# A three-layer graph convolution: each node's first 14 edges taken as lists by indirect fetches, in place of a search on TensorE and VectorE

## The chip, the cores and the metric

The kernel runs on one core of one Trainium2 chip. The metric is the device time of one execution in microseconds, and a kernel is stated by the median of its runs.

## The reference

6,250 nodes carry 256 features each. 100,000 edges (src, dst), sorted by dst, are the same in all three layers.

```python
deg = segment_sum(1, dst) + 1                 # the +1 is a node's own loop
dinv = rsqrt(deg)
h = x
for W, b in ((W1, b1), (W2, b2), (W3, b3)):   # 256 -> 512 -> 512 -> 256
    h = relu(segment_sum((h @ W)[src] * dinv[src] * dinv[dst], dst) + own loop + b)
out = layernorm(x + h)
```

The kernel aggregates before it multiplies by W, so that a layer gathers rows of its input table by src and sums them by dst.

## The kernel before

**Tiling.** The nodes are 50 blocks of 125 (`Q`); a block owns about 2,000 edges. A stage that counts comes first (the loop over `counted(g)`, ten blocks at a time): for each block it finds where each node's edges begin in the sorted list (`n_below`), the degrees, and dinv. Then three layers follow. In each, some blocks are *dense*: a matrix of edge counts between the block and each of the 50 source blocks, in uint8, is turned to float and multiplied with the table that lies in SBUF as two halves (`parts`). The other blocks are *gathered*: indirect fetches on the queue of GpSimd (POOL) bring the source rows of their edges.

**First layer** (`first_layer`). Blocks 0 to 20 are dense (L1453, 50 matmuls to a block). Blocks 21 to 49 are gathered, 16 fetches of 128 edges to a block and one row of rest edges for ten blocks (L1368). For blocks 26 to 45 the table holds both halves of a row, and a fetch lands in a slot of `split` (`SPLIT_ROWS[0]` of them, two more lent); for the others it lands in one of eight rows of `room`. The sum over edges is a matmul with a one-hot matrix (`product`, L1402; 17 to a block, 493 in all). Four one-hot matrices are made by one VectorE instruction (`more_hots`, L1324) into a tile of the pool `onehot`. One *chunk* is one fetch with all that the builder lays beside it; chunk c issues fetch c and multiplies what fetch c-5 brought (c-7 in the tail, from block 46 on).

**What else runs in the chunks of the first layer.** All of it is generators that are stepped once a chunk at build time, so that the order on each engine is fixed:

- `counts`: makes the uint8 matrices of blocks 0 to 25: one-hot pairs on VectorE (L1038), a matmul (L1111), a copy on ScalarE (L1072). It takes an accumulator bank from the shared list `common` when more than `SPARE` are in it.
- `after1`: turns, multiplies by W1, and stores a block's result to the table of layer 1 (L1673, L1705, L1713).
- `finding` (`all_found`): the numbers of the edges that the second and third layer fetch, for blocks 16 to 49, two blocks at a time. `found_rounds` computes `round_src`, the src of each node's first 14 edges (`ROUNDS`): a matmul that spreads the degrees (L600), a Sign on ScalarE, four matmuls with steps of the numbers (L609), a copy, and eight VectorE instructions (L617 to L632). `found_beyond` computes the numbers of the edges past the 14th. Both take a bank of `common`. `rows_risen` makes the steps they use.
- `caching`: once 20 dense blocks are done, loads the stored table of layer 1 into `parts`, two blocks every four chunks (L83).
- `teams`: blocks 0 to 15 of the second layer, dense, four at a time, 1,600 matmuls (L1197). They may start in the tail of the first layer when `counts` has stored 26 blocks and `found_beyond` is done, and go on in the second layer, where a goal per chunk steps them.

**Second and third layer** (`layer`). A gathered block has 14 fetches by `round_src`, one row per node, that VectorE adds up (L1631), and a few past them with one-hot matmuls (L1587). All are issued on POOL at L1571, 599 in the second layer and 317 in the third.

**Early in the program**, a step of `windows` also fetches from the edge list on POOL (L729) and VectorE reads the result at L736; `in_parts` then splits the rows of x that have been scaled by dinv (L899 on ScalarE, L900 on VectorE), and frees rows of `room` for the first fetches.

Of the kernel before, what the change touches and what calls it, by code (L numbers as in the profile page):

```python
# [10 lines left out]
F32 = mybir.dt.float32  # L11
# [3 lines left out]
I32 = mybir.dt.int32  # L15
# [23 lines left out]
SPLIT_ROWS = (7, 4, 7)  # L39
# [4 lines left out]
SPARE = 0  # L44
# [23 lines left out]
FIRST_EDGES = TEAM * TEAMS  # L68
G = 5
# [334 lines left out]
def sorted_path(ctx: ExitStack, tc: tile.TileContext, x, edges, starts, found, wts, biases, room, late, out):  # L404
# [41 lines left out]
    degs, before = ends[:Q], more[:Q]  # L446
# [55 lines left out]
    nodes_later = finder.tile([P, Q], BF16, name="elater")  # L502
    marks = [finder.tile([P, LANES], BF16, name=f"emarks{n}") for n in range(2)]
    less = finder.tile([P, KF], F32, name="eless")
    count_of = finder.tile([P, NE], BF16, name="ecount")
    low_of = finder.tile([P, NE, 2], BF16, name="elow")
    over_of = finder.tile([P, NE], BF16, name="eover")
    ends_of = finder.tile([P, NE], F32, name="eends")
    rises = finder.tile([P, NE, 2, 2 * KF + 1], BF16, name="erises")
    row_steps = [scratch[:, at:at + P // 2].bitcast(BF16) for at in (1456, 1984)]  # L510
# [4 lines left out]
    run = finder_room[:Q, 476:476 + 4 * KF].rearrange("p (b j) -> p b j", b=2)  # L515
    rounds_ready, beyond_ready = set(), set()

    def finder_numbers(spare):
# [11 lines left out]
        own, by, end_rows = spare[:, 2:5], spare[:, 5:7], spare[:, 7:8]  # L530
# [4 lines left out]
        nc.vector.tensor_scalar(nodes_later, number[:, :Q], part, None, op0=ALU.is_gt)  # L535
# [3 lines left out]
        nc.vector.tensor_single_scalar(by[:, 0:1], part, 1.0, op=ALU.add)  # L539
        nc.vector.tensor_single_scalar(by[:, 1:2], part, -1.0, op=ALU.add)  # L540
        nc.vector.tensor_scalar(eye, number, part, None, op0=ALU.is_equal)
        nc.vector.tensor_scalar(other, number, by[:, 0:1], None, op0=ALU.is_equal)
        nc.vector.tensor_sub(row_steps[0], eye, other)
        nc.vector.memset(eye[:, 0:1], 0.0)
        nc.vector.tensor_scalar(other, number, by[:, 1:2], None, op0=ALU.is_equal)
        nc.vector.tensor_sub(row_steps[1], other, eye)
# [32 lines left out]
    def rows_risen():  # L579

        for n in range(2):
            for b in range(0, NE, 16):
                of = slice(b, min(NE, b + 16))
                bank = yield from one_of_common(0)
                risen = bank[:, :(of.stop - b) * 2 * KF]
                nc.tensor.matmul(risen, lhsT=row_steps[n], rhs=bits[:, of].rearrange("p b k j -> p (b k j)"), start=True, stop=True)
                yield 1
                for k in range(2):
                    nc.scalar.activation(rises[:, of, k, 1 + n * KF:1 + (n + 1) * KF],
                                         risen.rearrange("p (b k j) -> p b k j", k=2, j=KF)[:, :, k], AF.Copy, scale=0.5)  # L590
# [1536 lines left out]
```

## Time and profile before

| | us |
|---|---|
| median of 3 runs | 2172.53 (2168.84 to 2179.11) |
| the profiled execution: its time | 2180.69 |
| the profiled execution: its span | 2178.6 |

| engine | busy us | share of the span |
|---|---|---|
| TensorE (PE) | 1877.0 | 86% |
| TensorE weight loads (PEld) | 1429.2 | 66% |
| VectorE (DVE) | 1584.5 | 73% |
| ScalarE (ACT) | 1120.9 | 51% |
| GpSimd (POOL) | 1437.7 | 66% |

The granted TensorE clock is a mean of 0.93 of full speed. Times in the views count from the span's start. The counting stage ends at about 88 us, where the first fetch of a table row is issued; the first layer's fetches end at 860 us, the second layer's start at 878 us. A row of the timeline gives the start, the duration, engine, line, what is written from what, the count of merged instructions, and in brackets how long the engine sat idle before and what ended it. A PE duration is modelled and overlaps the next matmul. "issue" is a short idle time that nothing in the profile explains. `w_sb` in the views is `scratch`, `st` a block's result, `sacc`, `smm`, `str`, `mat_ps`, `win_ps` the accumulator banks.

### The profile page before, as it was taken

What the parts mean: (1) busy time and instruction counts of PE and PEld (TensorE: products, weight loads), DVE (VectorE), ACT (ScalarE), POOL (GpSimd) and SP (SyncE); (2) the same over time, 40 slices, a digit from 0 to 9 for tenths busy, and PEclk for the clock granted to TensorE, in tenths of its full rate; (3) what the DMA queues carried; (4) which work ended last, traced back from release to release, by engine and by line L of the source; (5) the groups of instructions that cost most, each with busy time, mean ns of one, the idle gap of its engine ahead of it and who ended that gap; (6) DMA issues with size and microseconds to landing.
All of it is one profiled execution on the core that took longest, in us unless ns stands there. A gap on an engine that the chain in (4) does not pass through costs nothing.

```text
span 2178.6 us, 29385 instructions
## 1 busy us (share of the span) xinstructions
PE 1877.0 (86%) x8610; PEld 1429.2 (66%) x8610; DVE 1584.5 (73%) x3148; ACT 1120.9 (51%) x2138; POOL 1437.7 (66%) x1426
## 2 busy tenths in 40 slices
PE   3479999999999668789888997899886899999996
PEld 2366766666666346568666886678665677777775
DVE  6777777787876746667677676767666478888876
ACT  1566666777676445444434443434443455556552
POOL 2254655665666556677777777777774477777775
PEclk6599999999999779989999999999898999999998
DMA  7675677878879974777777777777788567787774
GB/s 165 185 220 182 174 209 199 219 208 209 215 212 265 306 206 140 222 201 222 216 223 208 216 220 204 215 220 217 210 228 227 153 167 206 199 208 206 201 211 135
DMA packets 226047, 449.46 MB, mean 206 GB/s; under 512 B 44089, under 2 KB 103426, under 8 KB 225876
## 3 DMA queue, kind: packets, MB, share of 16 engines
q0 software_dynamic: 117840, 303.15, 50.9%
q1 hardware_dynamic: 92196, 132.48, 21.8%
q10 hardware_dynamic: 15840, 11.86, 2.2%
q8 instruction: 69, 1.13, 0.2%
q14 instruction: 102, 0.84, 0.1%
HBM read 374.97 MB, written 69.81 MB: 204 GB/s over the span
## 4 chain that ended last, share of the span: by engine, by line
PE 43%; DMA 21%; DVE 13%; issue 9%; POOL 6%; ACT 4%; SPq 0%; ACTq 0%; POOLq 0%; DVEq 0%
DMA room<-tab,round_src 10%; POOL room L1571 6%; PE smm L1654 5%; PE sacc L1453 4%; DMA room<-tab,over_src 4%; PE sacc L1654 4%; PE str L1654 4%; DVE room L1038 4%; DMA room<-tab,efirst_src 2%; PE sacc L1402 2%; DMA halves<-both,efirst_src 2%; DVE total L1631 2%; PE smm L1789 2%; PE sacc L1587 1%; PE sacc L1705 1%
## 5 line engine op out<-in xcount | busy, mean ns | idle before, releaser
L1571 POOL DMA_INDIRECT room<-tab,round_src x728 | 762.4, 1047 | 280.1 <-issue 138.6
L1631 DVE TENSOR_TENSOR total<-total,room 125x512 f32<-125x512 f32 (+1 forms) x694 | 410.4, 591 | 116.6 <-DMA room<-tab,round_src 105.9
L1368 POOL DMA_INDIRECT halves<-both,efirst_src x304 | 286.9, 944 | 194.9 <-PE sacc L1402 51.9
L1038 DVE TENSOR_TENSOR room<-near_cols,slots 128x625 bf16<-128x625 f32 (+2 forms) x390 | 295.0, 802 | 28.0 <-PE sacc L1111 13.3
L1168 ACT CAST dense_rows<-parts 125x512 fp32r<-125x512 f32 x200 | 123.8, 619 | 252.8 <-PE near_cols L1197 250.5
L1571 POOL DMA_INDIRECT room<-tab,over_src x182 | 192.3, 1056 | 60.7 <-issue 29.6
L1368 POOL DMA_INDIRECT room<-tab,efirst_src x144 | 146.4, 1017 | 103.5 <-PE sacc L1402 28.8
L1170 DVE TENSOR_TENSOR dense_rows<-parts,dense_rows 125x512 fp32r<-125x512 f32 x200 | 137.9, 689 | 105.6 <-ACT dense_rows L1168 104.2
L1274 ACT CAST piece<-room 125x625 fp32r<-125x625 uint8 x217 | 152.2, 714 | 109.5 <-PE smm L1654 30.8
L1197 PE MATMUL sacc<-dense_rows 125*125 125x512 f32 x400 | 146.7, 441 | 60.6 <-DVE dense_rows L1170 25.9
L1453 PE MATMUL sacc<-parts,dense_rows 125*125 125x512 f32 x600 | 192.7, 428 | 2.7 <-ACT dense_rows L1274 2.5
L1623 ACT CAST halves<-room 128x512 fp32r<-128x512 f32 (+1 forms) x188 | 101.5, 545 | 173.5 <-DMA room<-tab,over_src 152.1
L1274 ACT CAST dense_rows<-room 125x625 fp32r<-125x625 uint8 x210 | 150.2, 719 | 38.0 <-PE sacc L1453 23.3
L1626 DVE TENSOR_TENSOR halves<-room,halves 128x512 fp32r<-128x512 f32 (+1 forms) x188 | 110.5, 597 | 69.1 <-ACT halves L1623 67.8
L1654 PE MATMUL smm<-parts,piece 125*125 125x512 f32 x550 | 141.7, 410 | 0.0
L1111 PEld LDWEIGHTS <-room 128*125 128x125 bf16 x650 | 89.3, 144 | 77.8 <-issue 47.4
L1197 PE MATMUL win_ps<-dense_rows 125*125 125x512 f32 x400 | 138.3, 428 | 1.5 <-DVE room L1750 1.5
L1197 PE MATMUL mat_ps<-dense_rows 125*125 125x512 f32 x400 | 138.5, 428 | 1.1 <-DVE room L1750 1.1
L1324 DVE TENSOR_TENSOR shot<-near_cols,edlo 128x500 fp32r<-128x500 f32 x108 | 72.8, 674 | 89.6 <-PE sacc L1402 45.9
L1197 PE MATMUL near_cols<-dense_rows 125*125 125x512 f32 x400 | 135.0, 419 | 1.9 <-DVE room L1750 1.9
L1654 PE MATMUL sacc<-parts,piece 125*125 125x512 f32 x505 | 127.6, 405 | 8.9 <-DVE piece L1274 8.9
L1197 PEld LDWEIGHTS sacc<-dense_rows 125*125 125x125 f32 x400 | 73.9, 191 | 91.5 <-DVE dense_rows L1170 35.8
(503 smaller groups left out, 4268.2 us busy)
## 6 DMA issues: line engine op xcount, KB each, us to landing
kept<-room SPq DMA_DIRECT2D x32, 683.6 KB
room<-kept SPq DMA_DIRECT2D x32, 683.6 KB
tab<-st SPq DMA_DIRECT2D x60, 224.0 KB
parts<-tab SPq DMA_DIRECT2D x29, 448.0 KB
room<-tab,round_src POOLq DMA_INDIRECT x728
both<-parts SPq DMA_DIRECT2D x10, 1120.0 KB
room<-kept SPq DMA_DIRECT2D x160, 68.4 KB
room<-in_x SPq DMA_DIRECT2D x50, 112.0 KB
```

Of the source, the lines that this page charges most:

```text
L1038: nc.vector.tensor_tensor(out, numbered[0][:, :shape[2]].unsqueeze(1).to_broadcast(shape), numbers.unsqueeze(2).to_broadcast(shape), op=AL ...
L1168: nc.scalar.copy(to[:, :HID], row)
L1170: nc.vector.tensor_sub(to[:, HID:], row, to[:, :HID].bitcast(F32))
L1197: nc.tensor.matmul(team_banks[n][:Q], lhsT=team_pieces[u % 2][:, n, :], rhs=both_parts[u % 2][:, h * HID:(h + 1) * HID], start=(u % NB == ...
L1274: convert(piece, matrix[:, c * PIECE:(c + 1) * PIECE, :])
L1368: nc.gpsimd.indirect_dma_start(out=row, out_offset=None, in_=table, in_offset=bass.IndirectOffsetOnAxis(ap=at, axis=0))
L1453: nc.tensor.matmul(acc_d[:Q], lhsT=got[done // PIECE][:, k % PIECE, :], rhs=parts[:, k], start=(k == 0), stop=(k == NB - 1))
L1571: nc.gpsimd.indirect_dma_start(out=row, out_offset=None, in_=tables[i], in_offset=bass.IndirectOffsetOnAxis(ap=at, axis=0))
L1623: nc.scalar.copy(two[:, :width], landed[chunk - hi_lag])
L1626: nc.vector.tensor_sub(two[:, width:], landed.pop(chunk - lo_lag), two[:, :width].bitcast(F32))
L1631: nc.vector.tensor_add(own, parts[:, b].bitcast(F32) if i == 1 and r == 0 else own, landed.pop(chunk - ADDED[i])[:Q])
L1654: nc.tensor.matmul(acc_d[:Q], lhsT=got[done // PIECE][:, k % PIECE, :], rhs=parts[:, k], start=(k == 0), stop=(k == NB - 1))
```

## The change

`n_below` already says where a node's edges begin, so the src numbers of its first 14 edges stand in 14 consecutive entries of the edge list. The changed kernel computes that place (`ask`) and fetches 28 words (14 pairs of src and dst) for each of the 125 nodes of a block with one indirect fetch (`asked`), 34 fetches in all. The first 18 blocks' lists are fetched in the counting stage into a tile of their own, the other 16 after the last fetch of the first layer, into a part of `room` that `found_beyond` used. `listed` turns lists into `round_src` with three VectorE instructions for many blocks. `found_rounds`, the tiles it needed, and half of `rows_risen` go. In the space that this frees the pool `onehot` has a third buffer and `split` in the first layer an eighth slot. `SPARE` goes from 0 to 1: `counts` leaves one bank in `common`.

```diff
-SPLIT_ROWS = (7, 4, 7)
+SPLIT_ROWS = (8, 4, 7)
-SPARE = 0
+SPARE = 1
+ASKED = 18
...
-    run = finder_room[:Q, 476:476 + 4 * KF].rearrange("p (b j) -> p b j", b=2)
+    late_lists = finder_room[:Q, :(NE - ASKED) * 2 * ROUNDS].bitcast(I32).rearrange("p (b r t) -> p b r t", r=ROUNDS, t=2)
...
     def rows_risen():
-        for n in range(2):
-            for b in range(0, NE, 16):
...
+        for b in range(0, NE, 16):
...
-    def found_rounds(e):
...
+    def asked(of, lists, first):
+        for e in of:
+            nc.gpsimd.indirect_dma_start(
+                out=lists[:, e - first].rearrange("p r t -> p (r t)"), out_offset=None, in_=edges,
+                in_offset=bass.IndirectOffsetOnAxis(ap=ask[:Q, e:e + 1], axis=0))
+
+    def listed(of, lists):
+        n = len(of)
+        es, bs = slice(of.start, of.stop), slice(FIRST_EDGES + of.start, FIRST_EDGES + of.stop)
+        real = scratch[:Q, 1536:1536 + n * ROUNDS].rearrange("p (b r) -> p b r", r=ROUNDS)
+        nc.vector.tensor_tensor(real, cols[:Q, :ROUNDS].unsqueeze(1).to_broadcast([Q, n, ROUNDS]),
+                                degs[:, bs].unsqueeze(2).to_broadcast([Q, n, ROUNDS]), op=ALU.is_lt)
+        nc.vector.scalar_tensor_tensor(real, lists[:, :n, :, 0], -float(N), real, op0=ALU.add, op1=ALU.mult)
+        nc.vector.tensor_single_scalar(round_src[:Q, es], real, float(N), op=ALU.add)
+        rounds_ready.update(of)
...
     def all_found():
         yield from rows_risen()
-        ahead = 1
-        for n in range(len(pairs_found) + ahead):
-            if n < len(pairs_found):
-                yield from found_rounds(pairs_found[n])
-            if n >= ahead:
-                yield from found_beyond(pairs_found[n - ahead])
+        for e in range(0, NE, 2):
+            yield from found_beyond(e)
...
+        lists = dp1.tile([Q, ASKED, ROUNDS, 2], I32, name="elists")
...
-                nc.scalar.copy(before[:, gs], n_below[:Q])
+                nc.vector.tensor_tensor(ask[:Q, es], n_below[:Q, skip:], line[:Q, g + skip:g + GRP], op=ALU.add)
+                asked(range(es.start, min(es.stop, ASKED)), lists, 0)
...
-                nc.scalar.copy(count_of[:Q, es], deg_ps[:, 1, skip:])
...
             bits_of(ed, find_space)
+            listed(range(ASKED), lists)
...
-    onehot = one.enter_context(tc.tile_pool(name="sonehot", bufs=2))
+    onehot = one.enter_context(tc.tile_pool(name="sonehot", bufs=3))
...
                 if chunk < total:
                     gather(chunk)
+                if chunk == total:
+                    asked(range(ASKED, NE), late_lists, ASKED)
...
     def last_weights():
+        listed(range(ASKED, NE), late_lists)
         load_w2()
```

How the order changes is shown at three places. In the changed file the first layer's lines stand 34 lower than before and the second layer's 32 lower: the gathers of L1368 are L1334, the products of L1402 are L1368, the teams of L1197 are L1163, L1571 is L1539, and the fetch of L729 is L692.

The first place is POOL's queue at the end of the counting stage, before the change (`ed` is the edges of a block, `room` the rows of the first table fetches, `w_sb` the window fetch):

```order
L774 DMA ed<-in_edges 128x32
L729 DMA w_sb<-in_edges,w_sb 125x256
L1368 DMA room<-tab_170,rest 128x256
L1368 DMA room<-tab_170,efirst_src 128x256 x36
L729 DMA w_sb<-in_edges,w_sb 125x256
L1368 DMA room<-tab_170,efirst_src 128x256 x44
```

The same place of POOL's queue after the change:

```order
L739 DMA ed<-in_edges 128x32
L590 DMA elists<-in_edges,eask 125x28 x18
L692 DMA w_sb<-in_edges,w_sb 125x256
L1334 DMA room<-tab_170,rest 128x256
L1334 DMA room<-tab_170,efirst_src 128x256 x36
L692 DMA w_sb<-in_edges,w_sb 125x256
```

The 18 list fetches stand ahead of the first window fetch, and so of all fetches of table rows.

The second place is POOL's queue where the first layer ends and the second begins, before the change:

```order
L1368 DMA halves_968<-both,efirst_src 128x512
L1368 DMA room<-tab_170,efirst_src 128x256 x64
L1571 DMA room<-tab_171,round_src 128x512 x14
L1571 DMA room<-tab_171,rest 128x512
L1571 DMA room<-tab_171,over_src 128x512 x4
```

The same place after the change:

```order
L1334 DMA halves_983<-both,efirst_src 128x512
L1334 DMA room<-tab_170,efirst_src 128x256 x64
L590 DMA room<-in_edges,eask 125x28 x16
L1539 DMA room<-tab_171,round_src 128x512 x14
L1539 DMA room<-tab_171,rest 128x512
```

The 16 late list fetches stand between the last gather of the first layer and the first of the second.

The third place is TensorE where the teams' matmuls begin in the tail of the first layer (`halves` are the fetched rows, `shot` the one-hot matrices, `dense_rows` the teams' operands). Before the change, with 428 products ahead of the first team row:

```order
L1402 MATMUL sacc_986<-halves_970,shot 125x512
L1402 MATMUL sacc_986<-halves_971,shot 125x512
L1197 MATMUL sacc_984<-dense_rows 125x512 x2
L1197 MATMUL win_ps<-dense_rows 125x512 x2
L1402 MATMUL sacc_986<-halves_966,shot 125x512
L1197 MATMUL mat_ps<-dense_rows 125x512 x2
```

After the change, with 454 products ahead of it:

```order
L1368 MATMUL sacc_999<-halves_982,shot 125x512
L1368 MATMUL sacc_999<-halves_983,shot 125x512
L1163 MATMUL mat_ps<-dense_rows 125x512 x2
L1368 MATMUL sacc_999<-halves_984,shot 125x512
L1163 MATMUL str<-dense_rows 125x512 x2
L1163 MATMUL win_ps<-dense_rows 125x512 x2
```

The teams begin 26 products later. Counted over the whole order up to the second layer's first matmul of W2, 302 team matmuls stand there, 372 before. Ahead of product 384 stand 998 dense matmuls of L1453 and 534 of the counting matmuls of L1111; before they were 1,050 and 575. The 1,000th dense matmul, after which `caching` may load, stood at product 366 before, with 550 counting matmuls ahead of it.

84 lines of the change are left out of this document (19 added, 65 removed).

## The prediction

> **What bounds the kernel now.** I read the stages first. These are rows of the windows view: busy time of each engine in a stretch (instructions in brackets), then the granted clock, the share of the DMA engines and their rate.
>
> ```profile
> core 0: us, PE busy (x) PEld busy (x) DVE busy (x) ACT busy (x) POOL busy (x), PEclk, DMA share, GB/s
> 95.00:200.00 105.00, 83.58 (x435) 63.08 (x435) 83.07 (x166) 64.99 (x128) 56.47 (x58) 0.88 0.74 228
> 200.00:640.00 440.00, 413.61 (x2228) 297.59 (x2227) 338.45 (x720) 303.51 (x585) 255.77 (x270) 0.99 0.76 201
> 640.00:700.00 60.00, 57.21 (x268) 41.79 (x267) 44.62 (x73) 41.87 (x73) 40.69 (x43) 1.00 0.98 264
> 700.00:800.00 100.00, 63.43 (x215) 38.85 (x213) 57.69 (x96) 43.89 (x85) 56.26 (x60) 0.76 1.05 265
> 800.00:877.00 77.00, 69.46 (x265) 50.36 (x266) 47.92 (x97) 47.18 (x108) 45.37 (x42) 0.96 0.55 150
> 877.00:1650.00 773.00, 679.93 (x2883) 535.49 (x2881) 547.22 (x847) 329.96 (x617) 596.22 (x569) 0.95 0.75 217
> ```
>
> The search that goes runs between 113 and 580 us, in the first layer. There TensorE is occupied 94% of the time (413.61 of 440) at full clock, and everything else has room. POOL issues a fetch every 1.63 us (440 over 270). From 700 us on the picture turns: DMA is full (1.05), TensorE has 37 us free in 100. In the second layer POOL sets the pace: 773 over 569 is 1.36 us to an instruction, close to the 1.25 between the starts of two undisturbed fetches (877.73 and 878.98, below). So a microsecond of TensorE's work is worth a microsecond up to about 700 us, and little behind that.
>
> Next, who waits for whom between 200 and 640 us; columns are total, times, longest, in us. The largest waits of VectorE and of TensorE:
>
> ```profile
> DVE shot L1324 <- PE sacc L1402: 30.9, 19, 3.9
> DVE shot L1324 <- PE mat_ps L1402: 10.0, 6, 2.9
> DVE shot L1324 <- PE str L1402: 9.9, 4, 3.9
> ...
> PE win_ps L1705 <- DVE st L1710: 4.9, 3, 3.3
> PE sacc L1673 <- DVE st L1710: 4.1, 2, 2.8
> PE win_ps L1111 <- ACT room L1072: 2.8, 2, 2.5
> PE sacc L1111 <- ACT room L1072: 2.6, 5, 1.4
> ```
>
> VectorE stands 51 us (three rows) before a one-hot tile whose buffer a product still reads, with everything queued behind it. TensorE's own waits are small, 14.4 us in these four rows: VectorE's stalls mostly wait for an engine that is late anyway.
>
> **The change, part by part.** *Search removed, TensorE.* What a matmul costs in the stream is the distance between starts:
>
> ```profile
> 300.69 0.28 PE L600 MATMUL str<-elater,ecount 125*128 125x125 bf16 x2
> 300.81 0.27 PE L1111 MATMUL win_ps<-room 128*125 128x250 bf16 x1
> 300.92 0.27 PE L1111 MATMUL smm<-room 128*125 128x250 bf16 x1
> 300.94 0.94 PE L1453 MATMUL sacc<-parts,dense_rows 125*125 125x512 f32 x3
> 301.72 0.39 PE L1402 MATMUL sacc<-dense_rows,shot 128*125 128x512 f32 x1
> 301.95 0.87 PE L1453 MATMUL sacc<-parts,dense_rows 125*125 125x512 f32 x3
> ...
> 302.89 0.19 PE L609 MATMUL str<-erises,eones 128*125 128x66 bf16 x1
> 302.92 0.22 PE L609 MATMUL str<-erises,ereached 128*125 128x66 bf16 x1
> ...
> 303.09 0.41 PE L1111 MATMUL win_ps<-room 128*125 128x250 bf16 x2
> ```
>
> Two of L600 take 0.12 us (300.69 to 300.81), four of L609 0.20 (302.89 to 303.09): 0.32 a pair of blocks, 17 pairs, 5.4 us. Three matmuls of `rows_risen` add under 1. I take 6. By durations it would be 17 x (2 x 0.14 + 4 x 0.22), about 20 us, and the gain 14 larger. I take the starts, because 0.22 lies over the next matmul in each of these rows. The Trainium skill, page "Perfetto Trace Analysis", section "Identifying the Most-Contended Engine", says likewise that matmul busy time misleads since instructions are pipelined; by that rule too the small figure is the one to use.
>
> *Search removed, VectorE and ScalarE.* One pair's eight instructions:
>
> ```profile
> 122.65 0.16 DVE L617 SCALAR_TENSOR_TENSOR eoff<-egot,more 125x2 f32<-125x2 f32 x1 [4.64 <-ACT egot L613]
> 122.72 0.23 DVE L618 SCALAR_TENSOR_TENSOR room<-egot 125x64 f32<-125x64 f32 x1
> ...
> 123.09 0.62 DVE L624 TENSOR_TENSOR w_sb<-room,ebegin 125x448 f32<-125x448 f32 x1
> ...
> 124.81 0.81 DVE L1038 TENSOR_TENSOR room<-near_cols,slots 128x625 bf16<-128x625 f32 x1
> ```
>
> That is 2.16 us (122.65 to 124.81), 37 us over 17 pairs, plus two ScalarE instructions each. Neither engine bounds the stage (338 and 304 of 440), so this counts only through TensorE's waits for them, under the buffers.
>
> *A spare bank.* With one bank left in the list, counting takes fewer chances. By the order, ahead of product 384 stand 52 dense matmuls and 41 counting matmuls fewer than before. At 0.26 (three of L1453 from 300.94 to 301.72) and 0.11 that is 13.5 + 4.5 = 18 us that leave the stretch where TensorE bounds and fall into the next 65 products, where it has 37 us of 100 free. I count the whole 18 as gained; if the tail takes them badly, half, 9. The teams, squeezed at the end, leave 70 matmuls (372 less 302), again 18 us, to the second layer. I count 2 there, because POOL bounds it and TensorE is free 12% (679.93 of 773); the ends are 0 and 18.
>
> *Third one-hot buffer, eighth slot.* The 51 us of VectorE stalls go for the most part. What is late next is TensorE itself, so of its 14.4 us I take half, 7; the ends are 0 and 14.
>
> *Early list fetches.* POOL's rows around the first table fetch and at the seam of the layers, a small indirect fetch from the same list (L819, a group of five: busy, mean ns), VectorE's `n_below` (L863) of blocks 20 to 29 and 30 to 39, and its use of L729:
>
> ```profile
> L819 POOL DMA_INDIRECT rest<-in_edges,place_i x5 | 4.8, 969 | 1.5 <-issue 1.2 <-DVE w L534 0.3
> 58.07 0.17 DVE L863 SCALAR_TENSOR_TENSOR n_below<-full_ps,n_part 126x10 f32<-126x10 f32 x1
> 69.57 0.17 DVE L863 SCALAR_TENSOR_TENSOR n_below<-full_ps,n_part 126x10 f32<-126x10 f32 x1
> 73.55 1.24 POOL L729 DMA_INDIRECT w_sb<-in_edges,w_sb  x1 [41.76 <-DVE w_sb L726]
> 79.59 0.22 DVE L736 TENSOR_SCALAR w_sb<-w_sb 125x128 f32<-125x128 int32 x1
> 87.94 3.31 POOL L1368 DMA_INDIRECT room<-tab,rest  x1 [13.15 <-DVE parts L900]
> ...
> 859.57 1.00 POOL L1368 DMA_INDIRECT room<-tab,efirst_src  x1 [0.30 <-issue]
> 877.73 0.94 POOL L1571 DMA_INDIRECT room<-tab,round_src  x1 [17.16 <-DMA parts<-st]
> 878.98 0.95 POOL L1571 DMA_INDIRECT room<-tab,round_src  x1 [0.30 <-issue]
> ```
>
> A list fetch costs POOL 0.97 + 0.30 = 1.27 us, or 1.54 if it is like L729. From 58.5 us ten run to 71.2, then four to 76.3, and L729 behind them starts 2.8 later than 73.55 (6.5 at the higher price). It had ended at 74.8 and was used without a wait at 79.59, so between 0 and 6.5 us reach VectorE, and by it `parts` and the first fetch; I take 1.2. `listed` adds three instructions of 252 columns, between 0.23 (L618) and 0.62 (L624) each: 0.7 to 1.9, I take 1.2. The four small VectorE additions and eight ScalarE copies of the counting stage cancel.
>
> *Late list fetches.* POOL idles from 860.6 to 877.7 for the last store. Sixteen at 1.27 take 20.3 us from 860.9 to 881.2: 3.5 us beyond the gap, 7.8 at the higher price, 0 if the gap widens. The second layer's rows for them are needed 18 blocks later, so `listed` there hides.
>
> *Sum:* -6 -18 -7 +2 +1.2 +1.2 +3.5 = -23 us against the profiled execution's 2180.7, of which 2178.6 is the span. That execution lies 8 above the median of 2172.5; the same difference on the median gives 2149.5, said as 2149.
>
> **The rivals.**
>
> *The tail keeps its length.* The loads of layer 1's table start when 1,000 dense matmuls are done:
>
> ```profile
> 681.49 0.79 SPq L83 DMA_DIRECT2D parts<-tab  x2
> ```
>
> From there to 877.73 are 196 us, with DMA full. That start moves from product 366 to 384, so TensorE's work up to it hardly falls: 18 products more at 0.23 (301.72 to 301.95), 16 counts less, the search's 6 less, about -4. With waits -7 and the additions of +8 the time is 2172.5 - 3, about 2170. For it speaks the DMA share of 1.05; against it that behind the later start only some 101 fetches remain in place of 121, and that rows of half the width come sooner.
>
> *TensorE's clock falls in the tail (slower).* In 700 to 800 us TensorE is idle for 37% and granted 0.76; in 800 to 877 the teams hold it at 0.96. The teams now start 26 products later. If the stage at 800 to 877 gets the clock of the one before it, its 69.46 us of work grow by 0.96/0.76, 18 us, and with the tail keeping its length the time is 2170 + 18 = 2188. It decides where the granted clock of the last 77 us falls below about 0.85; against it stand the delayed counts, which fill the same stretch. The Trainium skill, page "TensorE: Matmul & The Clock Gate", section "What's actually happening", has the clock at half after an idle window of about 3.4 us; the trace agrees in that 0.76 goes with the idle stretch.
>
> *All waits go.* TensorE's 14 us of waits vanish, and the teams' 18 us leave the tail as well: -6 -18 -14 -18 +8 = -48, 2124. Against it: landing fetches, not TensorE, hold the tail.
>
> **How the numbers follow.** Forecast 0.58, tail keeps its length 0.18, clock 0.13, all waits go 0.11. The forecast's own ends (half of the 18, no waits saved, both list prices high; or all waits saved and no cost at the seams) reach from about 2133 to 2167. The range takes in the first and third rival and leaves out most of the clock's: 2115 to 2178. A measurement of this kernel tells about 0.5%, 11 us, from no change. Faster by more than that, below 2161.6: nearly all of the forecast, 0.54, the third rival, 0.11, and some of the first, 0.05: 0.70. Slower: the clock, 0.13. The same: 0.17.
>
> **What would show it.** Right: POOL's fetches between 200 and 640 us come about 1.5 us apart; the waits of `shot` are nearly gone; the first table fetch stands at about 90 us; POOL's list fetches at the seam end 3 to 4 us after the point where the store would have let it go; the second layer's pace stays 1.36. The first load stands only some 10 us earlier, the first fetch of the second layer some 25. Wrong: the last fetch of the first layer not earlier than 850 us, a granted clock below 0.85 in the tail, or a second layer longer by 10 us.

## The result, and the profile after

The changed kernel takes 2108.53 us (median of 4 runs, 2099.89 to 2117.84), the kernel before 2174.1 in the same runs: a ratio of 0.970, 95% interval 0.965 to 0.975. That is faster, as forecast, but by some 65 us where 23 were forecast, and below the low end of 2115. The profiled execution took 2117.84, the longest of the four; its span is 2116.1 against 2178.6.

The stages first, in the windows view of the changed kernel (columns as before):

```profile
core 0: us, PE busy (x) PEld busy (x) DVE busy (x) ACT busy (x) POOL busy (x), PEclk, DMA share, GB/s
95.00:200.00 105.00, 80.64 (x478) 60.83 (x478) 84.02 (x164) 66.20 (x129) 59.83 (x57) 0.84 0.72 226
200.00:640.00 440.00, 437.45 (x2265) 324.16 (x2264) 338.44 (x641) 325.45 (x593) 301.65 (x319) 1.00 0.86 233
700.00:800.00 100.00, 70.02 (x250) 48.06 (x250) 69.18 (x139) 58.48 (x135) 63.04 (x61) 0.79 0.74 204
743.00:820.00 77.00, 62.97 (x238) 46.26 (x238) 37.87 (x75) 41.93 (x91) 50.22 (x44) 0.87 0.59 156
820.00:1593.00 773.00, 688.94 (x2932) 547.92 (x2932) 555.61 (x861) 339.36 (x632) 599.17 (x571) 0.95 0.76 218
```

Between 200 and 640 us TensorE is now occupied for 437 us of 440, where it was 414, and POOL issues 319 fetches there in place of 270: 1.38 us to a fetch, not 1.63. The second layer keeps its pace (571 POOL instructions in 773 us, before 569). The stretch from 743 to 820 us is the last ahead of the second layer, as 800 to 877 was before.

In the waits view of the changed kernel, 200 to 640 us, these four rows are all that TensorE waited for, 2.4 us, where the same view of before has 20 rows that add up to 25.5. For VectorE's one-hots the last line, a group of the page over the whole span, shows that hardly a wait is left:

```profile
PE sacc L1421 <- DVE szs L1653: 0.9, 1, 0.9
PE str L626 <- ACT epast L616: 0.8, 1, 0.8
PE sacc L1077 <- ACT room L1038: 0.5, 1, 0.5
PE sacc L1641 <- ACT room L1038: 0.2, 1, 0.2
...
L1290 DVE TENSOR_TENSOR shot<-near_cols,edlo 128x500 fp32r<-128x500 f32 x114 | 76.2, 669 | 4.3 <-PE smm L1368 2.9 <-PE sacc L1368 1.4
```

To see where the time went, I divided both executions at fetches of the first layer. The timeline of the changed kernel, POOL, with one VectorE row (L699 reads what L692 fetched): a list fetch, the window fetch, the first table fetch, the 33rd and the 353rd, the last, the first and last two late list fetches, the first fetch of the second layer.

```profile
59.73 1.21 POOL L590 DMA_INDIRECT elists<-in_edges,eask  x1 [2.71 <-DVE eask L836]
81.55 1.20 POOL L692 DMA_INDIRECT w_sb<-in_edges,w_sb  x1 [0.30 <-issue]
89.08 0.23 DVE L699 TENSOR_SCALAR w_sb<-w_sb 125x128 f32<-125x128 int32 x1 [8.44 <-DMA w_sb<-in_edges,w_sb]
97.44 3.29 POOL L1334 DMA_INDIRECT room<-tab,rest  x1 [14.68 <-DVE parts L865]
157.96 0.95 POOL L1334 DMA_INDIRECT room<-tab,efirst_src  x1 [0.63 <-PE sacc L1368]
616.25 0.94 POOL L1334 DMA_INDIRECT halves<-both,efirst_src  x1 [0.31 <-PE mat_ps L1421]
...
792.85 0.95 POOL L1334 DMA_INDIRECT room<-tab,efirst_src  x1 [0.30 <-issue]
794.11 1.25 POOL L590 DMA_INDIRECT room<-in_edges,eask  x1 [0.30 <-issue]
...
816.76 1.57 POOL L590 DMA_INDIRECT room<-in_edges,eask  x1 [0.30 <-issue]
818.64 1.19 POOL L590 DMA_INDIRECT room<-in_edges,eask  x1 [0.31 <-issue]
820.14 0.96 POOL L1539 DMA_INDIRECT room<-tab,round_src  x1 [0.31 <-DMA room<-in_edges,eask]
```

The 33rd and the 353rd fetch of the kernel before, from the same view of its trace:

```profile
151.49 0.95 POOL L1368 DMA_INDIRECT room<-tab,efirst_src  x1 [0.30 <-PE smm L1111]
...
678.93 0.94 POOL L1368 DMA_INDIRECT halves<-both,efirst_src  x1 [0.30 <-PE mat_ps L1111]
```

| piece, us | before | after | difference | forecast |
|---|---|---|---|---|
| start to the first table fetch | 87.9 | 97.4 | +9.5 | +2.4 |
| to the 33rd fetch | 63.6 | 60.5 | -3.0 | |
| 33rd to 353rd fetch | 527.4 | 458.3 | -69.2 | -31 (search 6, counting 18, waits 7) |
| to the last fetch of the first layer | 180.6 | 176.6 | -4.0 | 0 |
| seam, to the second layer's first fetch | 18.2 | 27.3 | +9.1 | +3.5 |
| rest | 1300.8 | 1296.0 | -4.8 | +2 |
| span | 2178.6 | 2116.1 | -62.5 | -23 |

So the gain was made in the stretch that TensorE bounds, and was more than twice what was forecast there. The two places where the lists are fetched cost 4 and 2.6 times their forecast, and this hid a part of it. The first of these figures holds for this execution: in the eight other profiled executions that have the same early lists and the usual pace, the first table fetch stands at 94.4 to 95.3 us, about 3 times the forecast.

To split the stretch I set against each distance between the starts of two matmuls the short one that its form shows where nothing holds it (0.23 us for a dense matmul or a product, 0.43 for L1705, 0.03 for a counting matmul), and call the rest the excess. Even in the changed kernel 61 us of it are left, most in pieces below 0.25 us, so only differences of it are read. Before: work 424.3, excess 103.0. After: work 397.1, excess 61.2. The work fell by 27 us, and 24 had been forecast (search 6, counting 18). The excess, which I read as TensorE's stalls, fell by 42, and 7 had been forecast. Other choices of the short distances from the same traces (by line, by form, by form and the one that follows) give 19 to 30 for the work and 39 to 50 for the excess, so a figure of this split is good to several us, and the stretch itself, for the one kernel that was profiled twice, to 1.

### The profile page after: what moved, and what is told of

The parts are those of the page before. It is cut to its first block, busy times and chain, and to the rows that moved or that the text cites. A ratio compares the mean times of both kernels' runs of the same rounds, so it can differ in the third digit from the quotient of the medians.

```text
span 2116.1 us, 29072 instructions
## 1 busy us (share of the span) xinstructions
PE 1845.0 (87%) x8505; PEld 1421.9 (67%) x8505; DVE 1549.6 (73%) x3017; ACT 1111.4 (53%) x2090; POOL 1477.4 (70%) x1460
## 5 line engine op out<-in xcount | busy, mean ns | idle before, releaser
L1539 POOL DMA_INDIRECT room<-tab,round_src x728 | 760.7, 1045 | 260.8 <-issue 139.4
L1334 POOL DMA_INDIRECT halves<-both,efirst_src x285 | 268.1, 941 | 126.4 <-issue 27.8
L1539 POOL DMA_INDIRECT room<-tab,over_src x182 | 192.9, 1060 | 59.6 <-issue 27.1
L1136 DVE TENSOR_TENSOR dense_rows<-parts,dense_rows 125x512 fp32r<-125x512 f32 x200 | 137.7, 688 | 103.0 <-ACT dense_rows L1134 102.8
L1334 POOL DMA_INDIRECT room<-tab,efirst_src x144 | 143.7, 998 | 98.1 <-PE sacc L1368 19.4
L1163 PE MATMUL mat_ps<-dense_rows 125*125 125x512 f32 x400 | 144.7, 437 | 59.5 <-DVE dense_rows L1136 28.7
L1240 ACT CAST dense_rows<-room 125x625 fp32r<-125x625 uint8 x210 | 147.1, 716 | 35.6 <-PE sacc L1421 19.4
L1555 PE MATMUL sacc<-halves,shot 128*125 128x512 f32 x400 | 133.7, 434 | 36.4 <-DVE halves L1594 19.2
L1594 DVE TENSOR_TENSOR halves<-room,halves 128x512 fp32r<-128x512 f32 (+1 forms) x188 | 111.2, 598 | 70.3 <-ACT halves L1591 69.1
L1163 PE MATMUL win_ps<-dense_rows 125*125 125x512 f32 x400 | 139.4, 431 | 0.7 <-DVE room L1718 0.7
L1622 PE MATMUL sacc<-parts,piece 125*125 125x512 f32 x550 | 139.6, 405 | 0.4 <-ACT piece L1240 0.4
L1163 PE MATMUL str<-dense_rows 125*125 125x512 f32 x400 | 139.4, 431 | 0.0
L1163 PE MATMUL near_cols<-dense_rows 125*125 125x512 f32 x400 | 137.0, 425 | 0.0
L1163 PEld LDWEIGHTS mat_ps<-dense_rows 125*125 125x125 f32 x400 | 76.4, 196 | 88.9 <-DVE dense_rows L1136 37.4
L1622 PE MATMUL mat_ps<-parts,piece 125*125 125x512 f32 x505 | 127.8, 405 | 8.9 <-DVE piece L1240 8.9
```

The costliest lines, as they stand in the source:

```text
L1136: nc.vector.tensor_sub(to[:, HID:], row, to[:, :HID].bitcast(F32))
L1163: nc.tensor.matmul(team_banks[n][:Q], lhsT=team_pieces[u % 2][:, n, :], rhs=both_parts[u % 2][:, h * HID:(h + 1) * HID], start=(u % NB == ...
L1240: convert(piece, matrix[:, c * PIECE:(c + 1) * PIECE, :])
L1334: nc.gpsimd.indirect_dma_start(out=row, out_offset=None, in_=table, in_offset=bass.IndirectOffsetOnAxis(ap=at, axis=0))
L1539: nc.gpsimd.indirect_dma_start(out=row, out_offset=None, in_=tables[i], in_offset=bass.IndirectOffsetOnAxis(ap=at, axis=0))
L1555: nc.tensor.matmul(acc[:Q, :size], lhsT=hots[b][:, k], rhs=two[:, c0:c0 + size], start=(k == c0 == 0), stop=(k == BEYOND + 1 and c0 + size ...
```

## The experiments

The kernel before ran beside each. In the table, "stretch" is the time from the 33rd to the 353rd fetch of the profiled execution and "excess" its part as above; for reference they are 527.4 and 103.0 before, 458.3 and 61.2 after.

| kernel | median | ratio to before, 95% | stretch | excess |
|---|---|---|---|---|
| the changed kernel again | 2112.46 | 0.973 (0.970 to 0.976) | 457.3 | |
| two one-hot buffers | 2121.80 | 0.976 (0.972 to 0.980) | 461.8 | 64.7 |
| seven slots | 2111.07 | 0.972 (0.967 to 0.978) | 459.6 | 61.4 |
| no spare bank | 2144.95 | 0.989 (0.984 to 0.995) | 484.1 | 69.1 |
| lists alone | 2157.30 | 0.994 (0.991 to 0.996) | 493.0 | 77.0 |
| before, spare bank alone | 2134.82 | 0.984 (0.979 to 0.990) | 490.1 | 94.9 |
| before, short one-hots | 2155.32 | 0.992 (0.989 to 0.994) | 509.6 | 84.9 |
| lists spread over the tail | 2108.79 | 0.971 (0.968 to 0.974) | 457.3 | |
| search's VectorE part put back | 2146.18 | 0.989 (0.985 to 0.993) | 488.2 | 88.1 |
| search's TensorE part put back | 2134.93 | 0.984 (0.979 to 0.988) | 475.9 | 78.7 |
| both parts put back | 2150.77 | 0.989 (0.986 to 0.993) | 485.9 | 95.2 |
| lists within the layer | 2121.06 | 0.976 (0.972 to 0.979) | 478.7 | |

### Undoing one part at a time

Four kernels, each the changed one with an edit: `bufs=3` to `bufs=2` for `onehot`; the eighth slot taken away; no spare bank; and all three undone, so that only the lists are left.

```diff
-    onehot = one.enter_context(tc.tile_pool(name="sonehot", bufs=3))
+    onehot = one.enter_context(tc.tile_pool(name="sonehot", bufs=2))
...
-SPLIT_ROWS = (8, 4, 7)
+SPLIT_ROWS = (7, 4, 7)
...
-SPARE = 1
+SPARE = 0
```

> The changed kernel (2108.5 us) with the one-hot pool back at two buffers; list fetches, eighth slot and spare bank stay. If the third buffer is what took away TensorE's stalls behind the products (about 44 us of the first layer that the prediction didn't count), the waits of VectorE for the one-hot tile come back to about 50 us or more between 200 and 640 us, the fetches go back from 1.38 towards 1.5 us or more, and the time is 2138 to 2155. If the search itself, with its VectorE and ScalarE steps, was what held TensorE, or if the spare bank did it, it stays at 2108 to 2118.

> The changed kernel with seven landing slots in the first layer in place of eight. If POOL's wait for a free slot (a fetch can't start before the product six fetches back has read its slot) matters, the time rises by 10 to 25 us, to 2118 to 2133. If only the one-hot buffer or the search matters, it stays within 5 us of 2108.5.

> The changed kernel with SPARE back at 0: counting takes the last bank again. The prediction put the later counting at 18 us of gain (9 if the tail takes it badly): 2118 to 2127. If the shift of dense and counting matmuls was the larger thing, 2140 or more. If a TensorE that no longer stalls makes the place of that work unimportant, within 5 us of 2108.5.

> The changed kernel with two one-hot buffers, seven slots and SPARE 0: only the lists in place of the search. If buffers and bank made the gain, the lists alone bring TensorE's 6 us and cost the 18 us that the counting stage and the seam grew by: about 2180. If the search was what held TensorE, 2120 to 2135.

This first set ran on a chip on which the kernel before took 2424.34 us, not 2174, so only its ratios are used: 0.985 (0.981 to 0.989), 0.986 (0.982 to 0.990), 0.991 (0.988 to 0.994) and 0.996 (0.993 to 0.999). The changed kernel itself was not run there, and times expected in us can't be held against these runs. The order already suggests that of the three parts the bank is worth most, and that the lists alone gain little. The same kernels were run again at the usual pace, with the changed kernel itself and two more:

> The changed kernel itself, unaltered, beside the kernel before on the same chip: 0.970 of it, between 0.965 and 0.975, if the chip is as in the first result. In the first four experiments the kernel before took 2424 us in place of 2174; where that comes back, the ratio shows what the change is worth under those conditions, and the first four are read against this one.

> The changed kernel with two one-hot buffers in place of three, once more, beside the changed kernel. If the third buffer ended TensorE's stalls, it is slower than the changed kernel by 30 to 45 us; if the search held TensorE, by less than 10.

> The changed kernel with seven landing slots. The third one-hot buffer turned out to be worth only about 9 us, though the waits of VectorE came back to 90 us without it; so about 40 us of the first layer have another cause. If it is the slot (POOL's fetch must wait for the product six back, and TensorE then waits for the fetch), this is 25 to 45 us slower than the changed kernel, ratio about 0.985 to 0.992 to the kernel before. If it is the search or the bank, within 10 us of it, ratio 0.972 to 0.977.

> The changed kernel with SPARE 0. If the later counting (and with it fewer matmuls beside each fetch while TensorE bounds) is the cause, 25 to 45 us slower than the changed kernel, ratio 0.985 to 0.992; by the prediction's own term 9 to 18 us, ratio 0.977 to 0.981; if slot or search is the cause, within 5 us of it.

> Only the lists in place of the search: two one-hot buffers, seven slots, no spare bank. If the search's chain held TensorE, ratio 0.975 to 0.985 (its gain less the 18 us that counting stage and seam grew by). If slot, bank and buffer made the gain, 0.995 to 1.005.

The slot is worth nothing (2111 against 2108.5 and 2112.5), as expected if search or bank is the cause. The third one-hot buffer is worth some 9 us by the medians, under the 10 named for the search; the intervals overlap. Without the spare bank the kernel is some 33 us slower, within the 25 to 45 named for the later counting. Its stretch is 25.8 us longer, 18.1 of it work (415.2 against 397.1), which is the 18 forecast, and 7.9 excess.

The lists alone are a miss: 0.994 lies outside the 0.975 to 0.985 named for the search, and just below the 0.995 named for slot, bank and buffer. They take 34 us from the stretch, 26 of them excess, so the search did hold TensorE, but they give 16 back at the counting stage and the seam (first table fetch at 95.05 us, seam 27.5). Beside one another the kernel before took 2174.66, the lists alone 2157.30, with third buffer and eighth slot 2144.95, and with the bank too, at seven slots, 2111.07. So by the whole time the bank is the largest step, and no part alone gives the gain.

What the two one-hot buffers do to the waits of the changed kernel, 200 to 640 us:

```profile
DVE shot L1290 <- PE sacc L1368: 37.7, 20, 4.8
DVE shot L1290 <- PE str L1368: 19.1, 12, 3.5
DVE shot L1290 <- PE smm L1368: 16.5, 8, 3.5
DVE shot L1290 <- PE win_ps L1368: 9.9, 6, 2.8
```

VectorE stands 83 us (four rows) before its one-hot tiles, more than before the change, and the stretch is only 3.5 us longer than with three buffers. Without the search these stalls do wait for an engine that is late anyway.

### The parts in the kernel before

The kernel before, once with the spare bank alone, and once with one-hot tiles of two matrices in four buffers, which take the same space and come free sooner.

```diff
-SPARE = 0
+SPARE = 1
...
-HOTS = 4
+HOTS = 2
...
-    onehot = one.enter_context(tc.tile_pool(name="sonehot", bufs=2))
+    onehot = one.enter_context(tc.tile_pool(name="sonehot", bufs=4))
```

> The kernel before, with the search, and only SPARE from 0 to 1. If the place of the counting matmuls is the cause, 20 to 45 us faster than the kernel before, ratio 0.979 to 0.991. If the search takes what the bank gives (the search holds a bank itself), or slot or search is the cause, ratio 0.993 to 1.005.

> The kernel before with the search, its one-hot tiles cut from 2 buffers of 4 matrices to 4 buffers of 2 in the same space: the tile that is written next was read six products ago or more, not four or fewer, at the price of about 140 VectorE instructions more. If VectorE's stand before the one-hot tile is what stalls TensorE, this gains 15 to 35 us on the kernel before, without lists, slot or bank. If the search's chain stalls TensorE, it gains nothing or loses up to 15.

The bank alone gains 1.6%, 34 us (22 to 45), more than any other part. Its stretch has 29 us less work, 8 less excess, and the tail did not pay: from the 353rd to the 465th fetch it took 172.0 us, before 178.1. This is the first case expected. The short one-hots gain 0.8%, about 18 us, at the low end of the 15 to 35 expected, all of it excess (103.0 to 84.9). So with the search in place VectorE's stalls were not free, as they are without it. The edit changes two things, though: the tiles come free sooner, and one instruction on VectorE is shorter (0.41 us for 0.68). Which of them counts was not separated.

### Which half of the search held TensorE

The changed kernel with two one-hot buffers, and per pair of blocks the eight VectorE instructions of `found_rounds` (on a tile of zeros), or its bank, six matmuls and two ScalarE instructions (on other operands), or both. Nothing uses what they compute.

```diff
         for e in range(0, NE, 2):
+            yield from search_tensor(e)
+            yield from search_vector(e)
             yield from found_beyond(e)
```

> The changed kernel with two one-hot buffers, and for each of the 17 pairs of blocks the eight VectorE instructions of the search put back, on a tile of zeros, at the chunk of the search where they stood; no matmul, no ScalarE instruction and no bank with them, and what they compute is used nowhere. Without them this kernel took 461.8 us from the 33rd to the 353rd fetch of the first layer, and 0.976 of the kernel before; the kernel before with a spare bank, whose search is whole, took 490.1. Theory V: the search held TensorE by VectorE's 37 us, which came ahead of one-hots that products needed; then the stretch grows by 20 to 28 us, to 482 to 490, and the ratio to about 0.986. Rival T: it held TensorE by its own matmuls, whose operands ScalarE makes, and by the bank it kept; then the stretch stays within 5 us of 462 and the ratio near 0.977.

> The changed kernel with two one-hot buffers, and for each of the 17 pairs the rest of the search put back on other operands: its bank, its six matmuls, the Sign and the copy on ScalarE, at the chunks where they stood; no VectorE instruction, and the result is used nowhere. Theory V: the stretch grows by the matmuls' own 5 us, to about 467, the ratio to 0.978. Rival T: it grows by 20 to 28 us, to 482 to 490, the ratio to about 0.986. If each half holds some, both kernels grow by some 10 to 18 us.

> The changed kernel with two one-hot buffers and both halves of the search put back, with nothing of it used. Whichever half it was, the stretch from the 33rd to the 353rd fetch should come back to about 490 us, and the ratio to about 0.988. If it stays below 480, the search cost something else, its place ahead of the search for the edges past the 14th or its wider steps; if it grows over 500, the copies are dearer than the original.

The timelines of POOL give the stretch, the 33rd and 353rd fetch, for the kernel without them, the VectorE part, the TensorE part and both, in this order:

```profile
154.72 1.02 POOL L1334 DMA_INDIRECT room<-tab,efirst_src  x1 [0.62 <-PE sacc L1368]
616.51 0.94 POOL L1334 DMA_INDIRECT halves<-both,efirst_src  x1 [0.30 <-PE mat_ps L1421]
```

```profile
159.31 0.95 POOL L1363 DMA_INDIRECT room<-tab,efirst_src  x1 [1.64 <-PE win_ps L1106]
647.55 0.94 POOL L1363 DMA_INDIRECT halves<-both,efirst_src  x1 [0.30 <-issue]
```

```profile
157.16 0.94 POOL L1358 DMA_INDIRECT room<-tab,efirst_src  x1 [1.65 <-PE smm L1101]
633.06 0.94 POOL L1358 DMA_INDIRECT halves<-both,efirst_src  x1 [0.57 <-PE mat_ps L1392]
```

```profile
158.32 0.94 POOL L1385 DMA_INDIRECT room<-tab,efirst_src  x1 [1.56 <-PE mat_ps L1419]
644.19 0.94 POOL L1385 DMA_INDIRECT halves<-both,efirst_src  x1 [0.31 <-PE str L1472]
```

Against 461.8 without them, the VectorE part adds 26.4 us, as Theory V says, the TensorE part 14.1, more than Theory V and less than Rival T allow, and both 24.1. Both together come to 485.9 with an excess of 95.2, and the kernel before with a spare bank, whose search is whole, has 490.1 and 94.9: the copies account for the search.

The three stretches do not hold the same work. Dense matmuls of `parts` in them: 910 without the copies, 896 with the VectorE part, 867 with the TensorE part, 863 with both. At 0.23 us each, 3, 10 and 11 us of work moved behind the stretch, so the TensorE part costs more than its 14.1. In excess the three add 23.4, 14.0 and 30.5; the other short distances give 27 to 29, 19 to 21 and 31 to 33. By the ratios the whole kernel grows by 28, 17 and 29 us, each ratio being good to some 8 us. So the VectorE part, which the prediction had put at nothing, alone costs nearly what both cost; the TensorE part costs something too, and the two do not add up.

One thing stands beside the instructions. Either part also adds five steps a pair to the generator, so that `found_beyond` is spread over more chunks: its last matmul with `emarks` stands at 485 and 480 us instead of 327. A kernel with the steps alone was not run. As the TensorE part has the same five, they cost at most what it lost, if nothing else in it gained; what the VectorE part lost beyond that, 9.4 us of excess (7 to 10 by the other distances), is then the least that is VectorE's own. With three one-hot buffers the parts were not put back.

How it holds TensorE is seen in the waits of the kernel with the VectorE part, 200 to 640 us, where these three rows name `emarks`, and in one place of the kernel before, VectorE's timeline and TensorE's at the same time:

```profile
PE mat_ps L642 <- DVE emarks L638: 3.1, 2, 2.5
PE str L642 <- DVE emarks L638: 2.2, 1, 2.2
PE sacc L642 <- DVE emarks L638: 1.8, 1, 1.8
```

```profile
334.58 0.15 DVE L617 SCALAR_TENSOR_TENSOR eoff<-egot,more 125x2 f32<-125x2 f32 x1
...
336.64 0.30 DVE L632 TENSOR_SCALAR round_src<-ereal 125x28 int32<-125x28 f32 x1
336.73 1.65 DVE L1038 TENSOR_TENSOR room<-near_cols,slots 128x625 bf16<-128x625 f32 x2
338.29 0.47 DVE L1685 SCALAR_TENSOR_TENSOR szs<-smm,sdinv,szs 125x256 f32<-125x256 f32 x1
338.68 0.57 DVE L641 TENSOR_SCALAR emarks<-elanes,eends 125x448 bf16<-125x448 f16 x2
```

```profile
336.11 0.94 PE L1453 MATMUL sacc<-parts,dense_rows 125*125 125x512 f32 x3
336.89 0.40 PE L1402 MATMUL win_ps<-halves,shot 128*125 128x512 f32 x1
339.07 0.36 PE L645 MATMUL sacc<-emarks,elow 128*128 128x448 bf16 x1 [1.78 <-DVE emarks L641]
339.27 0.27 PE L1111 MATMUL sacc<-room 128*125 128x250 bf16 x1
```

The search keeps VectorE from 334.58 to 336.73, 2.15 us, and the marks that TensorE's next matmul needs come that much later, behind two counting instructions and one that makes `szs`. TensorE starts nothing from 336.89 to 339.07: 2.18 us, where 0.23 is usual, so 1.95 are lost, nearly what the search took. This is one place; that the others go the same way is not shown row by row. The waits view calls 1.78 of it a wait, since it counts only from the product's modelled end; holes shorter than that overlap it does not show.

### Moving the list fetches

Twice the fetches were moved from the two places where they cost. Once 14 stay in the counting stage and 20 are spread over the last 110 fetches of the first layer. Once all 34 are issued within the layer, one every 8 chunks from chunk 40, in the space of the eighth slot.

```diff
-                if chunk == total:
-                    asked(range(ASKED, NE), late_lists, ASKED)
+                since = chunk - (total - LATE_FROM)
+                if since >= 0 and since % 5 == 0 and since // 5 < NE - ASKED:
...
+                    asked(range(ASKED + since // 5, ASKED + since // 5 + 1), late_lists, ASKED)
```

> The changed kernel with 14 early lists, so that none stands between the window fetch and its time, and the other 20 fetched one at a time every fifth fetch in the last 110 fetches of the first layer. The counting stage should lose its 9.5 us back by 5 to 8, the seam its 9 us back, and the tail pay 0 to 15 of POOL's 30 us for the 20 fetches: 0 to 15 us faster than the changed kernel. If POOL has no room in the tail, the same or up to 10 us slower.

> The changed kernel with seven slots of the split, and all 34 list fetches issued within the first layer: one every 8 chunks from chunk 40 on, 17 of them into a tile of their own, and after the numbers are taken from it the other 17 into the same tile, done by chunk 352. POOL is busy 69 per cent there and waits for slots. If the lists cost what they hold up, the first fetch comes at 86 to 88 us (97.4 in the changed kernel), the gap from the last fetch of the first layer to the first of the second is 18 us (27.3), the stretch from the 33rd to the 353rd fetch stays at 457 to 463, and the time falls by 13 to 19 us against the changed kernel, to a ratio of 0.964 to 0.966. Rival: what the seam gives is lost behind it, since the second layer has other work to end, as when the late lists were spread over the last 110 fetches (seam 9 us shorter, time the same); then only the 10 us at the start remain, a ratio near 0.968. If a list fetch holds the queue of fetches, the stretch grows by up to 34 x 1.5, 51 us.

Neither beats the changed kernel, and of the first the lower case, the same time, came true. POOL's timeline of the first shows the seam at 17.6 us, as before the change, and the first table fetch came at 87.4, but the tail took 186.5 us from the 353rd to the 465th fetch, not 173.7, and the total is the same (2108.79, where the changed kernel took 2112.46 in the same runs and 2108.53 in others):

```profile
792.26 0.94 POOL L1335 DMA_INDIRECT room<-tab,efirst_src  x1 [0.53 <-DVE halves L1394]
809.91 0.94 POOL L1542 DMA_INDIRECT room<-tab,round_src  x1 [16.70 <-DMA parts<-st]
```

The second also has its first fetch early (87.1) and a short seam (19.4), but its stretch is 478.7 us, 19 longer than with seven slots and the lists outside, although 66 dense matmuls fewer fall into it (847 for 913), and the whole is 10 slower. Its waits, 200 to 640 us:

```profile
PE sacc L1366 <- DMA halves<-both,efirst_src: 11.8, 10, 2.5
PE str L1366 <- DMA halves<-both,efirst_src: 3.7, 3, 1.5
PE win_ps L1366 <- DMA halves<-both,efirst_src: 3.5, 4, 1.5
```

TensorE waits 19.0 us for rows that have not landed; in the same view of the kernel before, of the changed one and of that with seven slots no row names a DMA. In the changed kernel POOL is busy for 302 us of 440 there, and its time was not free all the same. Expected was a ratio of 0.964 to 0.966, so this is a miss, by the third case named there.

## Why the prediction was right or wrong

**The step that failed** is "this counts only through TensorE's waits for them, under the buffers", with the term "waits, half, 7; the ends are 0 and 14". The search's 37 us on VectorE were put at nothing because VectorE was busy for 338 us of 440. Put back without the rest of the search, its eight instructions and their steps cost 26.4 us of stretch, 23 of them excess (88.1 less 64.7). The ScalarE instructions were put at nothing too, and the bank that the search holds was not priced: that half, without VectorE, costs 14.1 us or more, where 6 were counted for its matmuls. The cover that was named, the buffers, covers one-hots; it does not cover `emarks`, `st` and `szs`, which TensorE reads a moment after VectorE makes them. The Trainium skill, page "DVE: scalar operands, raw-bit mode, write accounting and state across instructions", section "5. Flops that outlive an instruction", calls VectorE's queue one in-order queue. The rows at 334.58 to 339.07 agree: what stood behind the search's 2.15 us on VectorE came later, and TensorE lost 1.95.

**The bound on it was none.** 14.4 us were the four largest rows of a view of 20 that add up to 25.5, and the view itself sees only idle time behind a matmul's modelled end. By the starts the stalls fell by 42. The prediction used starts for the matmuls' cost, and there it was right; it should have used them for the stalls as well.

**The sentence on VectorE's stalls** ("mostly wait for an engine that is late anyway") holds without the search (83 us of such waits, 3.5 us of stretch) and not with it (18 us of excess gone with short one-hots). Of the 42 us, undone in this order, 26 went with the search, 8 with buffers and slot, and 8 with the bank. Why the stalls cost only beside the search was not tested.

**The spare bank** was sized right where the order shows it: 18 us of work leave the stretch (measured 18.1), and the tail has room for them. The 8 us of stalls that it also takes were not seen, and for the whole kernel it is worth some 33 us (2144.95 without it), where 16 were forecast (18 less 2). Which waiting matmul a free bank lets go was not tested. The Trainium skill, page "Perfetto Trace Analysis", section "Matmul Optimizations", advises to use all eight accumulation banks. Here holding one back from counting gained 34 us, so it matters which work may take the last one.

**The search on TensorE**, 6 us by starts: with the lists alone the work of the stretch falls by 8.3 (424.3 to 416.0), near the 6 and far from the 20 of the durations. It is this run that speaks for the smaller figure; the rule that the prediction cites beside it, that matmul busy time misleads, does not by itself say which of two prices to take.

**The lists** were mis-sized. The answer on the line of the list fetches (duration: least, median, longest in ns; first and last start):

```profile
L590 POOL DMA_INDIRECT elists<-in_edges,eask x18: 1192/1198/2426, 50.0 to 80.1; - x18
L590 POOL DMA_INDIRECT room<-in_edges,eask x16: 1191/1228/1572, 794.1 to 818.6; - x16
```

With the 0.30 between two, a fetch costs 1.5 us by the median, the price "if it is like L729" (1.54), not the 1.27 that was taken from L819, and a few took longer. The window fetch starts 8.0 us later (81.55 for 73.55), VectorE waits 8.44 for it, and the first table fetch is 9.5 late; in the eight other executions it is 6.4 to 7.4 late, where 2.4 were forecast. The slack was misread as well: the prediction took 74.8, where the fetch's row on POOL ends, as the time from which VectorE could read, and saw 4.8 us of room up to 79.59. In the changed kernel VectorE stood waiting and could read 6.3 us after that row's end (82.75 to 89.08), in the other eight 3.9 to 4.5, so there was little room. The 16 late ones take 26 us from 794.11 to 820.14, 1.63 each, and the seam grows by 9.1, past the higher price of 7.8.

**The second layer** and all behind it got 4.8 us shorter instead of 2 longer, at the same pace, so a cost of the later teams does not show. The 4.8 are no finding: the changed kernel with seven slots, the same in these layers, has 1290.4 us there, the changed kernel 1296.0.

**The rivals.** "The tail keeps its length" did not hold. From the first load of layer 1's table to the second layer's first fetch were 196 us and are now 175, though the seam in it grew, and that load itself stands 37 us earlier than before (681.49), where 10 were named:

```profile
644.67 0.79 SPq L84 DMA_DIRECT2D parts<-tab  x2
```

TensorE's clock did fall where that rival said, in the last 77 us ahead of the second layer: 0.87, before 0.96, just above the 0.85 that was to decide. The whole still got faster. In 700 to 800 us it was 0.79 (before 0.76), and 0.95 in the second layer. "All waits go" is nearest in number (2124) and right that they go, but partly by luck: it too counted only 14 us of them, 8 of added cost where the two places cost 18.6, and 18 off the tail, where 4.0 went. Of the signs, the second layer's pace and the vanished `shot` waits came as named; the fetch pace (1.38 for 1.5), the first fetch (97.4 for 90), the second layer's first fetch (58 us earlier for 25) and the seam did not.

## What to carry to other kernels

Work that is taken from an engine that is not the busiest can be worth something where the bounding engine reads that engine's results soon after they are made, since its queue runs in order: look in the timeline for what stands behind the removed instructions and who waits for it. Measure the bounding engine's stalls by the distances between its starts, with the undisturbed distance of each form taken off, and not by the largest rows of the waits alone. Price a new fetch by the nearest row of the same shape, at its dearer end, and expect it to cost even where its queue looks a third idle: none of the three placings tried here was free.

## What the runs showed of the hardware

An indirect fetch of 112 bytes for each of 125 rows kept POOL as long (1.20 us) as the window fetch of 1 KB for each of 125 rows (1.20), and longer than one of a table row of 1 KB for each of 128 (0.94). So the issue did not get cheaper with the bytes; whether the count of rows makes the difference was not tested. The window fetch could be read by VectorE only 3.9 to 6.3 us after its row on POOL had ended. The waits that the profile names for TensorE were 25.5 us in 200 to 640, while the excess that went was some 42 in about the same stretch. And the same kernel before took 2424 us on one chip and 2170 to 2175 on the others, with the parts of the change in much the same order there; the cause was not looked for.
